# A gated Flamingo block on one core: the last two batch elements' ternary layers taken off GpSimd, their steps set apart, and reductions behind GpSimd pinned to their place

## The chip, the cores and the metric

The kernel runs on one core of a Trainium2 chip. A core has five engines that matter here: TensorE (PE; its weight loads, PEld, overlap its matmuls), VectorE (DVE), ScalarE (ACT), GpSimd (POOL) and SyncE (SP), which here only issues DMAs. Every engine works through its own queue in order; an instruction that waits for another engine holds up all that stands behind it on its own. The metric is the device time of one execution in microseconds (us); lower is better.

## The reference, cut to what matters

Four batch elements `x[b]` of 512 rows and 512 columns go through four layers, each added to the residual stream with a gate `tanh(g)`:

```python
x = x + tanh(g_xattn[0]) * wkv(layernorm(x), ctx)          # a scan over the rows
x = x + tanh(g_ffn[0])   * bitlinear_ffn(layernorm(x))     # 512 -> 2048 -> 512, 1-bit weights
x = x + tanh(g_xattn[1]) * attention(layernorm(x), ctx)    # 16 heads; int8-rounded projections
x = x + tanh(g_ffn[1])   * ternary(layernorm(x))           # RMS norm, int8 rounding, 512x512
```

The change is in the last two lines. The attention ends in a projection of its output, per row: the row's largest magnitude gives a scale, the row is rounded to integers, multiplied with the integer weights `wp`, rescaled and added to `x`. The ternary layer does nearly the same: normalise a row (`layernorm`, then RMS norm), multiply by `gamma`, take the largest magnitude, round to integers, multiply with ternary weights, rescale, add to `x`, write out.

## The kernel before, in words

**Tiles and lines of work.** One element `xb` is four tiles `t` of 128 rows x 512 columns. The work is written as Python generators ("lines"), each for one layer of one element, that yield after every small step. `run` (L1158) always advances the line whose next step has the smallest `place`; a line's `parts` say over which stretch of places its steps are spread. Places are counted in slots: `SLOTS = NT * NF + 1 = 17` slots to one element's feed-forward layer. So element b's attention runs beside element b+1's feed-forward layer, and the last element's attention (`alone`, b = 3) runs beside nothing but what is left of element 2: its `project_out` and its ternary layer. After the last attention unit only element 3's own end is left (`end`, L1045): `project_out` and `ternary` for tiles 0 and 1, and a step behind them for tiles 2 and 3.

**Who sets the order.** The matmuls and transposes of TensorE are chained to each other in the order of the steps (`in_turn`, `next_turn`, L153 to L165), so TensorE's order is the written one. On the other engines a scheduler in the build sets the order, by its own estimate of when operands are ready; `tc.keep_in_program_order(ins)` takes one instruction out of that freedom: it stays behind the instruction that was written just ahead of it on its engine. Before the change only some `bn_stats` have this (`pinned=True` in `layernorm`, L209).

**The attention** works in units of one head pair and half of the rows (`units`, L925; 16 units an element). Each unit has four score matmuls (`s_ps`), a row maximum on VectorE (`at_nm`, L938), an exponential on ScalarE (`at_P`, L940), sixteen transposes (`pt_ps`), copies of them out of PSUM on ScalarE (L960) or, for the last element, half of them on VectorE (L958), the product with the values (`o_ps`, one group of matmuls a unit) and a small collecting step (L998). `prepared` (L850) makes the rounded queries of a tile: normalise on GpSimd (`centred_aside`, L228), largest magnitude on VectorE (`absmax`, L231), round on ScalarE (`rounded`, L246), transpose on TensorE.

**`project_out`** (L1015), a tile: `absmax` of the output row block, scale, `rounded`; four transposes (`qr_ps`) and a copy; four matmuls (`p_ps`); then on VectorE `at_y` (L1031), and the addition to `xb` (L1032) on VectorE for the last element and on GpSimd for the others.

**`ternary`** (L1103), a tile, from statistics made by `layernorm(..., rms=True)`: for elements 0 to 2 the row is normalised on GpSimd (L228) and multiplied by `gamma` there (L1110); for element 3 on ScalarE (L224) and VectorE. Then on VectorE `absmax` (L231) and four small operations on one column (L1115 to L1118) that give the scale; `rounded` on ScalarE (L246); four transposes (`qr_ps`), a copy out (L253), four matmuls (`f_ps`), the addition to `xb` (L1128) and the DMA out. `layernorm` itself is per tile a `bn_stats` (L207) and a `bn_aggr` (L210), then for all of its tiles together two small operations for the variance (L213, L214), eleven of `rsqrt` (L182: a first guess by integer arithmetic and three Newton rounds of three operations each) and two that form scale and offset (L219, L220).

**Places.** Element b's attention ends at `end`; its `project_out` takes the six steps up to `end + 2.4` slots, and the ternary layer of elements 0 and 1 the seven steps from `end + 3` to `end + 8` slots, that of element 2 from `end + 4.5` to `end + 12` slots, with `aside=True` (each step late in its slot).

Of the kernel before, what the change touches and what calls it, by code (L numbers as in the profile page):

```python
# [10 lines left out]
F32 = mybir.dt.float32  # L11
# [10 lines left out]
P = 128  # L22
# [8 lines left out]
def kernel(  # L31
# [150 lines left out]
    def rsqrt(v, n):  # L182
# [13 lines left out]
            y = y2  # L196
        return y

    def layernorm(xb, rms=False, tiles=range(NT), pinned=False):

        n = len(tiles)
        mv = sm.tile([P, n, 2], F32, name="mv", tag="mv")
        for i, t in enumerate(tiles):
            s6 = sm.tile([P, 6], F32, name="s6", tag="s6")
            stats = nc.vector.bn_stats(s6, xb[:, t, :])  # L207
# [12 lines left out]
        nc.vector.scalar_tensor_tensor(r[:, 1, :], mv[:, :, 0], -1.0, y, ALU.mult, ALU.mult)  # L220
        return {t: (r[:, 0, i : i + 1], r[:, 1, i : i + 1]) for i, t in enumerate(tiles)}
# [5 lines left out]

        nc.gpsimd.tensor_scalar(dst, xb[:, t, :], r[t][0], r[t][1], ALU.mult, ALU.add)  # L228

    def absmax(dst, src):  # L230
        nc.vector.tensor_reduce(dst, src, AX.X, ALU.max, apply_absolute_value=True)  # L231

    def quantise(dst, src, rscale, lo, hi=127.0):

# [596 lines left out]
    def attention_layer(b, xb, pool, tiles=range(NT)):  # L831
# [18 lines left out]
        def prepared(t, r):  # L850
            xn = row("at_xn")
            centred_aside(xn, xb, r, t)
            s = sm.tile([P, 2], F32, name="at_s", tag="at_s")
            yield True
            absmax(s[:, 0:1], xn)
            int8_scale(s[:, 0:1], s[:, 1:2], s[:, 0:1])
            rounded(xn, s[:, 1:2])
            yield True
            transposed_rows(xqT[:, :, t * P : (t + 1) * P], xn)
            sp = bank("sx_ps")[:, 0:P]  # L860
            transpose(sp, s[:, 0:1].to_broadcast([P, P]), ident)
# [153 lines left out]
        def project_out(t):  # L1015
            s = sm.tile([P, 2], F32, name="at_s", tag="at_s")
            o = o_all[:, t, :]
            absmax(s[:, 0:1], o)
            int8_scale(s[:, 0:1], s[:, 1:2], s[:, 0:1])
            rounded(o, s[:, 1:2])  # L1020
            yield True
            oqT = pool.tile([P, NC, P], BF16, name="at_oqT", tag="at_oqT")
            transposed_rows(oqT, o)
            yield True
            pp = bank("p_ps")
            for c in range(NC):
                matmul(
                    pp, lhsT=oqT[:, c, :], rhs=wpT[:, c, :], start=(c == 0), stop=(c == NC - 1)
                )
            y = row("at_y")  # L1030
            nc.vector.scalar_tensor_tensor(y, pp, s[:, 0:1], swp_b, ALU.mult, ALU.mult)  # L1031
            (nc.vector if alone else nc.gpsimd).tensor_tensor(  # L1032
                xb[:, t, :], xb[:, t, :], y, ALU.add
            )
            yield True
# [9 lines left out]
        def end(ts):  # L1045

            yield from together([project_out(t) for t in ts])
            r = layernorm(xb, rms=True, tiles=ts)
            yield from together([ternary(b, xb, pool, t, r) for t in ts])


        ahead, behind_it = end((0, 1)), end((2, 3))
# [47 lines left out]
            yield from in_steps([project_out(t) for t in tiles], 1)  # L1100


    def ternary(b, xb, pool, t, r):  # L1103

        last = b == NB - 1
        if r is None:
            r = layernorm(xb, rms=True, tiles=[t])
        xn = pool.tile([P, D], F32, name="tf_xn", tag="at_row", bufs=ROWS)
        (centred if last else centred_aside)(xn, xb, r, t)
        (nc.vector if last else nc.gpsimd).tensor_tensor(xn, xn, gamma_b, ALU.mult)  # L1110
        s = sm.tile([P, 3], F32, name="tf_s", tag="tf_s")
        if not last:
# [15 lines left out]
        nc.vector.scalar_tensor_tensor(xt, fp, s[:, 2:3], xt, ALU.mult, ALU.add)  # L1128
# [238 lines left out]
```

## Time and profile before

| | |
|---|---|
| time, median of 3 runs | 1129.53 us (1128.88 to 1131.5) |
| the profiled execution: its own time | 1129.12 us |
| its span, first to last instruction | 1127.3 us |
| mean granted TensorE clock | 0.954 of full |
| busy, share of the span | PE 85%, DVE 78%, ACT 64%, POOL 27% |
| the last element's attention and the end | from about 955 us to the end |
| the end alone, after the last attention unit | from about 1089 us to the end |

The span is 1.82 us shorter than the execution's own time, and this execution is 0.41 us under the median. Busy shares are averages over stages with different limits; what one stage is worth has to be read in that stage. In the lines of the profile, `L171` is the transposing helper and `L168` the matmul helper, so those go by their tiles (`qr_ps`, `pt_ps`, `p_ps`, `f_ps`). Similarly L231 is `absmax` and L246 `rounded`, wherever they are called.

### The profile page before, as it was taken

The page shows a single profiled execution, that of the slowest core. Times are in us where ns is not written, and L with a number is a line of the kernel's source. Part 1 is how long each engine was busy: PE and PEld are TensorE (multiplying, and loading weights), DVE is VectorE, ACT ScalarE, POOL GpSimd, SP SyncE. Part 2 cuts the span into 40 slices and gives each one's busy share as a digit, 9 for nine tenths or more (in the row PEclk, how much of TensorE's full clock was granted, in tenths as well). Part 3 has the DMA queues.
Part 4 walks back from the last instruction along what each step waited for, and adds up shares of the span by engine and source line. Part 5 has one row for each costly group of instructions (what it writes and reads, how often), then busy time and mean ns, then how long its engine had stood idle before and what let it go on. Part 6 is the DMA issues. An engine that isn't in the chain of part 4 may idle for free.

```text
span 1127.3 us, 16575 instructions
## 1 busy us (share of the span) xinstructions
PE 962.9 (85%) x5548; PEld 678.1 (60%) x5548; DVE 877.7 (78%) x1885; ACT 721.4 (64%) x1482; POOL 308.8 (27%) x301
## 2 busy tenths in 40 slices
PE   3878898988878978899998797999999899888983
PEld 2344565555546656676776475777777677555651
DVE  5857547769877799998769899978689766688776
ACT  5677655453224677667767676777676677877763
POOL 3821004333104143531215536212122400112000
PEclk9888999998888999999999999999999999998996
DMA  8188854443434654645555554464674572333401
GB/s 279 38 291 302 295 193 150 177 177 149 149 120 151 225 189 155 217 159 175 191 187 182 164 182 169 152 208 150 218 214 146 187 233 60 113 104 104 130 2 38
DMA packets 85668, 189.58 MB, mean 168 GB/s; under 512 B 12240, under 2 KB 36816, under 8 KB 74576
## 3 DMA queue, kind: packets, MB, share of 16 engines
q1 hardware_dynamic: 85584, 188.53, 49.7%
q8 instruction: 44, 0.72, 0.3%
q14 instruction: 40, 0.33, 0.1%
HBM read 148.65 MB, written 39.85 MB: 167 GB/s over the span
## 4 chain that ended last, share of the span: by engine, by line
PE 43%; DVE 29%; ACT 13%; issue 5%; POOL 4%; DMA 4%; SPq 1%; ACTq 0%; POOLq 0%; DVEq 0%
PE ff_hp L168 13%; PE ff_acc L168 6%; PE pt_ps L171 5%; PE o_ps L168 4%; DVE at_nm L938 3%; PE v_ps L168 3%; DVE wk_q L631 3%; PE s_ps L168 3%; ACT at_P L940 3%; DVE qg_i L671 2%; PE tp_ps L171 2%; ACT at_PT L960 2%; PE qr_ps L171 2%; ACT wk_e L603 1%; DMA wn<-in_L_ffn_w_dram 1%
## 5 line engine op out<-in xcount | busy, mean ns | idle before, releaser
L168 PE MATMUL ff_hp<-wT,xp 128*128 128x512 f32 x1024 | 272.3, 410 | 3.1 <-ACT at_P L940 2.1
L168 PEld LDWEIGHTS ff_hp<-wT,xp 128*128 128x128 f32 x1024 | 195.4, 195 | 51.9 <-ACT at_P L940 4.4
L940 ACT ACTIVATE at_P<-s_ps,at_nm 128x512 f32<-128x512 f32 x256 | 174.8, 690 | 64.8 <-DVE at_nm L938 63.4
L938 DVE TENSOR_REDUCE at_nm<-s_ps 128x1 f32<-128x512 f32 x256 | 165.8, 677 | 27.1 <-PE s_ps L168 26.7
L676 POOL TENSOR_TENSOR ff_z<-qg_b,qg_s 128x512 f32<-128x512 bf16 x64 | 71.2, 1112 | 378.9 <-ACT qg_b L675 326.3
L171 PE MATMUL pt_ps<-ident,at_P 128*128 128x128 f32 x1024 | 142.0, 279 | 12.5 <-ACT at_os L980 5.1
L960 ACT COPY at_PT<-pt_ps 128x512 f32<-128x512 f32 x224 | 125.0, 596 | 39.1 <-PE pt_ps L171 38.4
L171 PEld LDWEIGHTS pt_ps<-ident,at_P 128*128 128x128 f32 x1024 | 113.9, 141 | 54.7 <-issue 13.9
L168 PE MATMUL ff_acc<-wT,hr 128*128 128x512 f32 x512 | 136.7, 408 | 6.3 <-DVE hr L688 3.3
L168 PE MATMUL s_ps<-at_kR,at_qR 128*128 128x512 f32 x256 | 97.2, 448 | 19.9 <-ACT at_P L940 12.7
L168 PEld LDWEIGHTS ff_acc<-wT,hr 128*128 128x128 f32 x512 | 92.4, 190 | 27.4 <-DVE hr L688 4.6
L736 ACT ACTIVATE ff_z<-ff_hp,coef 128x512 f32<-128x512 f32 x64 | 43.9, 686 | 68.7 <-PE ff_hp L168 65.6
L168 PE MATMUL o_ps<-at_PT,at_V 128*32 128x256 f32 x1024 | 72.6, 397 | 1.6 <-ACT at_PT L960 0.9
L675 ACT CAST qg_b<-qg_i 128x512 bf16<-128x512 int8 x80 | 49.4, 617 | 34.2 <-DVE qg_i L671 24.7
L741 DVE SCALAR_TENSOR_TENSOR ff_z<-ff_hp,coef,ff_z 128x512 f32<-128x512 f32 x64 | 47.6, 744 | 28.3 <-PE ff_hp L168 28.1
L168 PE MATMUL v_ps<-wkvT,cT 128*128 128x512 f32 x128 | 63.4, 643 | 5.0 <-DVE wT L318 1.8
L168 PEld LDWEIGHTS s_ps<-at_kR,at_qR 128*128 128x128 f32 x256 | 45.6, 194 | 35.9 <-ACT at_P L940 20.7
L168 PE MATMUL k_ps<-cT,wkvT 128*128 128x512 f32 x128 | 62.3, 637 | 3.1 <-ACT cT L455 1.4
L737 DVE SCALAR_TENSOR_TENSOR ff_z<-ff_z,ff_hp 128x512 f32<-128x512 f32 x64 | 43.5, 679 | 25.7 <-ACT ff_z L736 25.7
L687 ACT CAST hr<-tp_ps 128x512 fp32r<-128x512 f32 x64 | 37.6, 588 | 33.9 <-PE tp_ps L171 33.9
L631 DVE RECIPROCAL wk_q<-wk_q 128x256 f32<-128x256 f32 x32 | 54.3, 1718 | 1.4 <-POOL wk_p L619 1.4
L171 PE MATMUL tp_ps<-ident,ff_z 128*128 128x128 f32 x256 | 40.3, 281 | 14.9 <-ACT at_PT L960 5.8
(177 smaller groups left out, 1749.7 us busy)
## 6 DMA issues: line engine op xcount, KB each, us to landing
wT<-wD SPq DMA_DIRECT2D x72, 1024.0 KB, 5.3
wn<-in_L_ffn_w_dram SPq DMA_DIRECT2D x18, 1024.0 KB, 7.3
at_kR<-kD SPq DMA_DIRECT2D x128, 128.0 KB, 3.5
at_qR<-qD SPq DMA_DIRECT2D x256, 64.0 KB, 2.2
wD<-wT SPq DMA_DIRECT2D x12, 1024.0 KB, 4.5
kD<-k_half SPq DMA_DIRECT2D x16, 512.0 KB, 3.3
qD<-at_half SPq DMA_DIRECT2D x32, 256.0 KB, 2.1
cn<-in_ctx_dram SPq DMA_DIRECT2D x8, 512.0 KB, 5.9
```

The costliest lines, as they stand in the source:

```text
L168: return in_turn(nc.tensor.matmul(*args, **kwargs))
L171: return in_turn(nc.tensor.transpose(*args))
L631: nc.vector.reciprocal(half, half)
L675: nc.scalar.copy(qb, qi)
L676: nc.gpsimd.tensor_tensor(grouped(src), grouped(qb), s.unsqueeze(2).to_broadcast([P, NG, GS]), ALU.mult)
L687: nc.scalar.copy(part[:, 0, :], pt)
L736: nc.scalar.activation(z, hp, AF.Tanh, scale=coef[:, 0:1])
L737: nc.vector.scalar_tensor_tensor(z, z, 1.0, hp, ALU.add, ALU.mult)
L741: nc.vector.scalar_tensor_tensor(z, hp, coef[:, 1:2], z, ALU.mult, ALU.mult)
L938: nc.vector.tensor_reduce(nm, sp, AX.X, ALU.max, negate=True)
L940: nc.scalar.activation(lanes[k, i, t], sp, AF.Exp, bias=nm, accum_out=sums[k][:, t, i : i + 1],)
L960: made[k] = nc.scalar.copy(dst, blocks(pt))
```

## The change

1. **Element 2 and 3, the addition in `project_out`.** The addition to `xb` is on VectorE for both (it was on GpSimd for element 2), and `at_y` gets a buffer of another pool instead of one of the three row buffers that the attention uses.
2. **Element 2 and 3, statistics.** A new function `statistics` in place of `layernorm`: pinned `bn_stats`, the same `rsqrt`, but the mean and the scale are handed on apart. For element 3's tiles 2 and 3 the three Newton rounds are done on GpSimd, four operations each (`rsqrt_aside`).
3. **Element 2 and 3, the ternary layer.** One VectorE instruction, `(x - mean) * gamma`, takes the place of the normalising and the multiplication; it and the magnitude don't need the scale, which enters only the small column operations afterwards. Buffers come from pools that the feed-forward layer has left. The step that ended after the GpSimd work is gone.
4. **Element 2's places.** `project_out` is spread from `end - 0.15` to `end + 4.65` slots (to `end + 2.4` before), the ternary layer from `end + 4.85` to `end + 11.85` slots without `aside`; its statistics are a step of their own.
5. **Elements 0 and 1, and all of `prepared`.** `absmax` of what GpSimd has made, and the `bn_stats` of the ternary layer, are pinned to their place.

```diff
+    def rsqrt_aside(v, n):
+        half = sm.tile([P, n], I32, name="rs_half", tag="rs_half")
+        nc.vector.tensor_scalar(half, v.bitcast(I32), 1, None, ALU.logical_shift_right)
+        y = sm.tile([P, n], F32, name="rs_y", tag="rs_y")
+        nc.vector.tensor_scalar(y.bitcast(I32), half, -1.0, float(0x5F3759DF), ALU.mult, ALU.add)
+        for _ in range(3):
+            t = sm.tile([P, n], F32, name="rs_t", tag="rs_t")
+            nc.gpsimd.tensor_tensor(t, v, y, ALU.mult)
+            nc.gpsimd.tensor_tensor(t, t, y, ALU.mult)
+            nc.gpsimd.tensor_scalar(t, t, -0.5, 1.5, ALU.mult, ALU.add)
+            y2 = sm.tile([P, n], F32, name="rs_y", tag="rs_y")
+            nc.gpsimd.tensor_tensor(y2, y, t, ALU.mult)
+            y = y2
+        return y
...
-    def absmax(dst, src):
-        nc.vector.tensor_reduce(dst, src, AX.X, ALU.max, apply_absolute_value=True)
+    def absmax(dst, src, pinned=False):
+        ins = nc.vector.tensor_reduce(dst, src, AX.X, ALU.max, apply_absolute_value=True)
+        if pinned:
+            tc.keep_in_program_order(ins)
...
 # prepared
-            absmax(s[:, 0:1], xn)
+            absmax(s[:, 0:1], xn, pinned=True)
...
 # project_out
-            y = row("at_y")
+            if b > NB - 3:
+                y = wk.tile([P, D], F32, name="at_y", tag="wk_v")
+            else:
+                y = row("at_y")
             nc.vector.scalar_tensor_tensor(y, pp, s[:, 0:1], swp_b, ALU.mult, ALU.mult)
-            (nc.vector if alone else nc.gpsimd).tensor_tensor(
+            (nc.vector if b > NB - 3 else nc.gpsimd).tensor_tensor(
                 xb[:, t, :], xb[:, t, :], y, ALU.add
             )
...
 # end
-            r = layernorm(xb, rms=True, tiles=ts)
-            yield from together([ternary(b, xb, pool, t, r) for t in ts])
+            means, scale = statistics(b, xb, ts)
+            yield from together([ternary(b, xb, pool, t, means, scale) for t in ts])
...
+    def statistics(b, xb, tiles):
+        n = len(tiles)
+        mv = sm.tile([P, n, 2], F32, name="mv", tag="mv")
+        for i, t in enumerate(tiles):
+            s6 = sm.tile([P, 6], F32, name="s6", tag="s6")
+            tc.keep_in_program_order(nc.vector.bn_stats(s6, xb[:, t, :]))
+            nc.vector.bn_aggr(mv[:, i, :], s6)
+        v = sm.tile([P, n], F32, name="ln_v", tag="ln_v")
+        nc.vector.tensor_scalar(v, mv[:, :, 1], LN_EPS, RMS_EPS, ALU.add, ALU.mult)
+        nc.vector.tensor_tensor(v, v, mv[:, :, 1], ALU.add)
+        y = rsqrt_aside(v, n) if b == NB - 1 and tiles[0] else rsqrt(v, n)
+        m = sm.tile([P, n], F32, name="ln_m", tag="ln_m")
+        nc.vector.tensor_scalar(m, mv[:, :, 0], -1.0, None, ALU.mult)
+        at = {t: slice(i, i + 1) for i, t in enumerate(tiles)}
+        return {t: m[:, at[t]] for t in tiles}, {t: y[:, at[t]] for t in tiles}
...
 # ternary
-        last = b == NB - 1
-        xn = pool.tile([P, D], F32, name="tf_xn", tag="at_row", bufs=ROWS)
-        (centred if last else centred_aside)(xn, xb, r, t)
-        (nc.vector if last else nc.gpsimd).tensor_tensor(xn, xn, gamma_b, ALU.mult)
+        last = b > NB - 3
+        if last:
+            xn = ff.tile([P, D], F32, name="tf_xn", tag="ff_a", bufs=3)
+        else:
+            xn = pool.tile([P, D], F32, name="tf_xn", tag="at_row", bufs=ROWS)
...
+        if last:
+            nc.vector.scalar_tensor_tensor(xn, xb[:, t, :], r[t], gamma_b, ALU.add, ALU.mult)
+            absmax(s[:, 0:1], xn)
+            nc.vector.tensor_scalar(s[:, 0:1], s[:, 0:1], scale[t], 1e-5, ALU.mult, ALU.add)
+        else:
+            centred_aside(xn, xb, r, t)
+            nc.gpsimd.tensor_tensor(xn, xn, gamma_b, ALU.mult)
             yield True
-        absmax(s[:, 0:1], xn)
-        nc.vector.tensor_scalar(s[:, 0:1], s[:, 0:1], 1e-5, None, ALU.add)
+            absmax(s[:, 0:1], xn, pinned=True)
+            nc.vector.tensor_scalar(s[:, 0:1], s[:, 0:1], 1e-5, None, ALU.add)
         nc.vector.reciprocal(s[:, 1:2], s[:, 0:1])
-        nc.vector.tensor_scalar(s[:, 1:2], s[:, 1:2], 127.0, None, ALU.mult)
+        if last:
+            nc.vector.tensor_scalar(s[:, 1:2], s[:, 1:2], scale[t], 127.0, ALU.mult, ALU.mult)
+        else:
+            nc.vector.tensor_scalar(s[:, 1:2], s[:, 1:2], 127.0, None, ALU.mult)
...
-        xT = pool.tile([P, NC, P], BF16, name="tf_xT", tag="at_oqT")
+        if last:
+            xT = ring.tile([P, NC, P], BF16, name="tf_xT", tag="w")
+        else:
+            xT = pool.tile([P, NC, P], BF16, name="tf_xT", tag="at_oqT")
...
 # ternary_layer
-        r = layernorm(xb, rms=True)
-        yield from in_steps([ternary(b, xb, pool, t, r) for t in range(NT)], 1)
+        if b == NB - 2:
+            r, scale = statistics(b, xb, range(NT))
+            yield
+        else:
+            r, scale = layernorm(xb, rms=True, pinned=True), None
+        yield from in_steps([ternary(b, xb, pool, t, r, scale) for t in range(NT)], 1)
...
 # the places of the lines
-            (end, end + 2.4 / SLOTS, 6),
+            (end, end + 2.4 / SLOTS, 6)
+            if b != NB - 2
+            else (end - 0.15 / SLOTS, end + 4.65 / SLOTS, 6),
...
-                (end + (3 if b < NB - 2 else 4.5) / SLOTS, end + (8 if b < NB - 2 else 12) / SLOTS, 7),
-                aside=True,
+                (end + 3 / SLOTS, end + 8 / SLOTS, 7)
+                if b < NB - 2
+                else (end + 4.85 / SLOTS, end + 11.85 / SLOTS, 7),
+                aside=b < NB - 2,
```

Counted over the built programs, VectorE has 4 instructions fewer (1887 to 1883), ScalarE 4 fewer, GpSimd as many as before (12 of 128x512 go, 12 of 128x2 come), and TensorE and SP as many. TensorE's written order differs only in the stretch of element 2's `project_out`.

More of the change, by code (lines that the diff above doesn't have):

```diff
@@ L197, in rsqrt @@
         return y
+    def rsqrt_aside(v, n):
+        half = sm.tile([P, n], I32, name="rs_half", tag="rs_half")
+        nc.vector.tensor_scalar(half, v.bitcast(I32), 1, None, ALU.logical_shift_right)
+        y = sm.tile([P, n], F32, name="rs_y", tag="rs_y")
+        nc.vector.tensor_scalar(
+            y.bitcast(I32), half, -1.0, float(0x5F3759DF), ALU.mult, ALU.add
+        )
+        for _ in range(3):
[7 more added lines that the diff above has]
+        return y
     def layernorm(xb, rms=False, tiles=range(NT), pinned=False):
@@ L1100, in attention_layer @@
             yield from in_steps([project_out(t) for t in tiles], 1)
-    def ternary(b, xb, pool, t, r):
-        last = b == NB - 1
-        if r is None:
-            r = layernorm(xb, rms=True, tiles=[t])
-        xn = pool.tile([P, D], F32, name="tf_xn", tag="at_row", bufs=ROWS)
-        (centred if last else centred_aside)(xn, xb, r, t)
-        (nc.vector if last else nc.gpsimd).tensor_tensor(xn, xn, gamma_b, ALU.mult)
-        s = sm.tile([P, 3], F32, name="tf_s", tag="tf_s")
-        if not last:
+    def statistics(b, xb, tiles):
[13 more added lines that the diff above has]
+        return {t: m[:, at[t]] for t in tiles}, {t: y[:, at[t]] for t in tiles}
@@ new lines, in ternary @@
+    def ternary(b, xb, pool, t, r, scale=None):
+        last = b > NB - 3
[3 more added lines that the diff above has]
+            xn = pool.tile([P, D], F32, name="tf_xn", tag="at_row", bufs=ROWS)
+        s = sm.tile([P, 3], F32, name="tf_s", tag="tf_s")
+        if last:
+            nc.vector.scalar_tensor_tensor(
+                xn, xb[:, t, :], r[t], gamma_b, ALU.add, ALU.mult
+            )
+            absmax(s[:, 0:1], xn)
[3 more added lines that the diff above has]
+            nc.gpsimd.tensor_tensor(xn, xn, gamma_b, ALU.mult)
@@ L1113, in ternary @@
             yield True
-        absmax(s[:, 0:1], xn)
-        nc.vector.tensor_scalar(s[:, 0:1], s[:, 0:1], 1e-5, None, ALU.add)
+            absmax(s[:, 0:1], xn, pinned=True)
+            nc.vector.tensor_scalar(s[:, 0:1], s[:, 0:1], 1e-5, None, ALU.add)
         nc.vector.reciprocal(s[:, 1:2], s[:, 0:1])
-        nc.vector.tensor_scalar(s[:, 1:2], s[:, 1:2], 127.0, None, ALU.mult)
+        if last:
+            nc.vector.tensor_scalar(
+                s[:, 1:2], s[:, 1:2], scale[t], 127.0, ALU.mult, ALU.mult
+            )
+        else:
+            nc.vector.tensor_scalar(s[:, 1:2], s[:, 1:2], 127.0, None, ALU.mult)
```

## The prediction

> **What bounds the kernel now.** I read the waits first, because the change takes GpSimd out of the way of VectorE. Columns: waiting engine and line, whom it waited for, us in total, times, longest.
>
> ```profile
> DVE tf_s L231 <- POOL tf_xn L1110: 6.0, 6, 2.3
> DVE at_s L231 <- POOL at_xn L228: 4.4, 4, 1.7
> DVE s L207 <- POOL xb L1032: 3.2, 4, 1.4
> PE qr_ps L171 <- ACT tf_xn L246: 17.6, 4, 8.0
> PE qr_ps L171 <- ACT at_o L246: 7.6, 3, 3.4
> ```
>
> VectorE stands at a magnitude or a statistic until GpSimd has made the row; TensorE stands at the transposes of a row until it is rounded (14.0 of the 17.6 lie in the end, 3.6 in element 2). The waits are worth what stands behind them, so next the stages: windows cut at the starts of `o_ps`, one attention unit each. Columns: window, us, then busy us (and instructions) of PE, PEld, DVE, ACT, POOL, then granted clock, DMA share, GB/s.
>
> ```profile
> 982.03:998.01 15.98, 12.20 (x70) 7.57 (x69) 11.91 (x26) 12.97 (x31) 1.26 (x1) 0.83 0.52 162
> ...
> 1021.34:1026.66 5.32, 4.76 (x42) 3.19 (x41) 4.64 (x19) 4.21 (x13) 0.00 (x0) 1.00 0.72 209
> 1026.66:1036.64 9.98, 6.31 (x45) 4.20 (x45) 7.55 (x29) 6.05 (x16) 6.62 (x7) 0.84 0.36 104
> 1036.64:1044.41 7.77, 7.45 (x49) 4.99 (x49) 5.39 (x14) 5.86 (x15) 1.45 (x2) 0.77 0.00 0
> 1044.41:1050.60 6.19, 6.11 (x49) 4.03 (x48) 4.89 (x10) 5.43 (x14) 0.00 (x0) 1.00 0.28 87
> ```
>
> A plain unit takes 5.32 us; one that carries a tile of the ternary layer 6.19. Element 2's `project_out` (first row) and the start of its ternary layer (third and fourth) are far over that, at a lower clock. The timeline says why (start, us, engine, line, operation; in brackets the idle time before and its releaser):
>
> ```profile
> 883.75 0.69 DVE L231 TENSOR_REDUCE tf_s<-tf_xn 128x1 f32<-128x512 f32 x1 [2.26 <-POOL tf_xn L1110]
> ...
> 1034.51 0.69 DVE L231 TENSOR_REDUCE tf_s<-tf_xn 128x1 f32<-128x512 f32 x1 [0.72 <-POOL tf_xn L1110]
> 1034.74 1.12 PE L171 MATMUL qr_ps<-ident,tf_xn 128*128 128x128 f32 x4 [3.59 <-ACT tf_xn L246]
> ```
>
> Last the end, in the chain of waits (start, us, what):
>
> ```profile
> 1102.19 0.82 ACT tf_xn L224
> ...
> 1108.03 0.82 ACT tf_xn L246
> ...
> 1113.72 0.82 ACT tf_xn L224
> ...
> 1117.59 0.82 ACT tf_xn L246
> ...
> 1123.20 0.75 DVE xb L1128
> ```
>
> From the first `at_y` (1095.05) to 1113.7 the chain is VectorE nearly throughout, step after step: statistics and Newton rounds of tiles 0, 1, their rows, then the same for tiles 2, 3.
>
> **Prices.** On VectorE a 128x512 operation occupies 0.60 us (L207 at 1097.10, L1032 at 1097.70), 0.66 from PSUM, and its dependent starts 0.76 after it; a column operation occupies 0.07, its dependent starts 0.20 later (1099.36, 1099.56). A rounding is 0.82, four cold transposes 1.1, the copy 0.7, four cold `f_ps` matmuls 1.4, the last addition 0.75.
>
> **The end.** In the built order VectorE now runs, from 1095.05: four `at_y` (2.64), and fourteen 128x512 operations (8.4): four additions, four `bn_stats`, three rows, three magnitudes. In between stand about 23 column operations, mostly free to follow at once: 2.3. So the guess for tiles 2, 3 is there at 1095.05 + 13.35 = 1108.4. The roundings of tiles 0, 1 start about 1109.0 and 1109.7, 2.4 and 1.7 us later than before; that costs nothing as long as their TensorE work (done about 1114.5) is ahead of tile 3's. Then twelve dependent GpSimd steps, while VectorE stands at the first column operation that needs their scale; queued behind it are the whole of tile 3's row and magnitude, so the wait is on the path. The trace has no GpSimd arithmetic of two columns. Nearest rows: its 128x1 memset, 0.10, plus 0.08 between dependent GpSimd operations (884.95 for 0.78, next at 885.81): 0.18 a step. From above: 1.27 and 0.77 for 128x512, with the 0.08 1.35 and 0.85: nine and three of them, 14.7 in all. I take 0.25, near the memset because the size is near: 3.0 us, so 1111.45. Behind it: column operations 0.55, row 0.75, magnitude 0.7, column operations 0.55 (2.55), rounding 0.82, transposes 1.1, copy 0.7, `f_ps` 1.4, addition 0.75, handoffs 0.1: 7.4. The last addition ends at 1118.85, not 1123.95: **-5.1**. The bounds: 0.18 gives -5.9, 14.7 gives +6.6; the turning point is 0.67 a step.
>
> The rule that speaks against this step is in the Trainium skill, GPSIMD Engine Reference, section 3.1: elementwise work belongs on VectorE, since a GpSimd instruction passes two software dispatch hops. From its 4497 ns for 2048 elements at 2.5 to 2.6 cycles of 1.2 GHz I estimate 0.06 to 0.23 us of fixed cost; by that the twelve steps would take about 0.7 to 2.8 us, and no row here shows it. The page also names contention with VectorE for SBUF; here VectorE stands still meanwhile.
>
> **Element 2, project_out.** GpSimd loses four additions (1.28 each), VectorE gains them: 4 x 0.60 = 2.4. It loses the four `bn_stats` here (2.7), which move to the ternary layer's first step. So VectorE's load is about even, and the 2.9 us in which TensorE waited for a rounded `at_o` inside 982 to 998, and the 1.8 in which VectorE waited for GpSimd's addition, are spread away. The 2.6 us wait for `at_qR`'s DMA at 979 stays. TensorE in a plain unit: 4.76; transposes add 0.45, `p_ps` 1.0, `q_ps` 0.95. The six units from 982.03 to 1026.66 took 44.6. In the new order they carry: transposes, `q_ps` and one more score pair (9.8; before, that far took 9.3); two tiles' transposes and products (7.8); one (6.3); `p_ps` and `q_ps` (6.7); nothing (5.35, twice): 41.3, **-3.3**. Bounds: 0 if VectorE fills the units (it is busy 5.26 of 5.35 in 1015.99 to 1021.34), -8 if all over the plain sum goes.
>
> **Element 2, ternary layer.** GpSimd loses 4 x 0.774 and 4 x 1.287. VectorE gains four rows, 2.5, and the four `bn_stats`. Six units from 1021.34 to 1062.88 took 41.5. After: the statistics lengthen one unit to 6.5; the next, with a row and a magnitude, 6.1; then the built order has three rows, two magnitudes and about eleven column operations ahead of a row maximum, 4.5 us during which the exponentials and TensorE run dry: 8.5; then 6.5, 6.3, 5.9: 39.8, **-1.7**, bounds +3 (that block as long as today's 9.98 and 7.77 stay, statistics on top) and -4. The new row from two SBUF tiles has no row of its own; its neighbours are 0.69 (L1110) and 0.75 (L1128).
>
> **Elements 0 and 1.** From 880 to 906 VectorE waits 5.1 us for GpSimd's rows, and TensorE 3.6 behind it (3.2 at one place). Pinned, these magnitudes come after their unit's own work. The first tile's stands about 1.3 us of VectorE work behind the scale, while GpSimd needs 0.77 + 1.29: a new wait of 0.8, queued behind it a row maximum. 3.6 less 0.8, less something for later roundings: **-2.0**, bounds -3.6 and +2. At element 0's layer (655 to 700) VectorE is busy 44.5 of 45 and waits for no GpSimd row, so there only the new 0.8 counts; in `prepared` three waits of 0.9 go. Together **0**, bounds -3 and +3.
>
> Sum: -5.1 - 3.3 - 1.7 - 2.0 = -12.1; 1129.1 - 12.1 = 1117.0 for an execution like the profiled one, and 0.4 more for the median: **1117.4**. Its own range, with the middle values of the bounds, is 1111 to 1122.
>
> **Rivals.**
> *VectorE is the bound of the last attention* (20%): it gains 4.9 us of 128x512 work there, the units are 90% and more VectorE, and what GpSimd's waits give, the work takes back. Then the end alone counts: 1124.4. For it: 5.37 of 5.63 in 1005.00 to 1010.63. Against it: 4.7 to 4.9 of about 6 in the units from 1044 on.
> *Pinned magnitudes make TensorE wait for roundings* (13%), the case on the other side. A magnitude that stands at its place comes later, its rounding too, and TensorE's order is fixed. `project_out`'s magnitudes are late already, and there TensorE waits 7.6 us for 16 tiles, 0.48 a tile; for `prepared` only 3.4, for elements 0 and 1's ternary rows nothing. 24 tiles are newly pinned. From 0.5 us a tile it eats the whole 12.1; at 0.7 it costs 16.8: 1134.1. Against it: those rows have a unit or more of lead.
> *GpSimd's small steps cost like large ones* (7%): +6.6 in place of -5.1: 1129.1, no change. Against it: the 0.10 memset.
> *More than the sum* (10%): with the waits gone the clock stays at 1.00 from 980 to 1050 and the 11 us that TensorE idles or runs slow there go as well: about 1110.
>
> Clock: the rows above show 0.84 and 0.77 after a wait of 3.6 us. The Trainium skill, TensorE: Matmul & The Clock Gate, Part 1, puts the limit at an idle window of about 3.4 us; if waits stay under it, 1.3 us of the 7.77 unit's matmuls would go in any case, which is inside the sum above.
>
> **Numbers.** The forecast 50%: 1117.4. A measurement of this kernel can tell 0.2%, 2.3 us, from no change. Faster: the forecast, the first and the last rival, less a little that ends near zero: 0.77. Same: the third and that little: 0.09. Slower: 0.14. From 1109 to 1130 only most of the second rival and half of the last are left out.
>
> **What would show it.** After: no VectorE wait for `tf_xn` or `xb` by GpSimd past 950 us; units from 982 to 1063 of 8.5 at most but the first; GpSimd steps of 0.2 to 0.3 in the end, about 24 us from the first `at_y` to the last addition (28.9 before). Wrong if `qr_ps` waits for `tf_xn` or `at_xn` grow before 950, if units with rows stay at 8 to 10 us, or if GpSimd's steps are over 0.67.

## The result, and the profile after

The change makes the kernel slower: 1150.9 us, median of 5 runs (1146.66 to 1153.12), against 1129.65 us (1128.88 to 1132.19) for the kernel before beside it. The ratio is 1.0168, with a 95% interval of 1.0138 to 1.0199; the forecast was 1117.4, and its range ended at 1130. The profiled execution, the slowest of the five, has a span of 1151.3 us (1127.3 before) and a mean granted clock of 0.938 (0.954).

In the changed kernel's lines, `absmax` is L250 (L231 before), `rounded` L267 (L246), the normalising on GpSimd L246 (L228). First the waits, the answer to the five lines that the prediction began with (waiting engine and line, whom it waited for, us in total, times, longest):

```profile
DVE tf_s L250 <- POOL tf_xn L1162: 4.5, 3, 2.2
DVE at_s L250 <- POOL at_xn L246: 0.9, 1, 0.9
PE qr_ps L171 <- ACT tf_xn L267: 25.0, 5, 11.0
PE qr_ps L171 <- ACT at_xn L267: 7.9, 3, 4.2
PE qr_ps L171 <- ACT at_o L267: 4.7, 2, 3.4
```

The change does what it says: VectorE's waits for GpSimd's rows fall from 13.6 us to 5.4 (2.6 come new, for the Newton rounds in the end). But TensorE's waits for a rounded row grow from 28.6 (17.6, 7.6 and the 3.4 of `at_xn`) to 37.6. These totals can't say where the 24 us of span went, because a wait early in TensorE's order delays everything behind it.

So I matched the TensorE instructions of the two traces, which are the same ones in nearly the same order, and took for each how much later it starts than in the trace of before. That difference rises in steps. Table 1 gives the steps by stage (us, worked out from the starts in the traces; the columns are stages in the time of before). The lower rows are the experiments that follow. Where exactly a stage is cut moves a step by up to 0.9 us.

| kernel | 340 to 385: element 0's queries | 660 to 710: element 0's ternary layer | 860 to 900: element 1's ternary layer | 977 to the end: elements 2 and 3 |
|---|---|---|---|---|
| after | +6.2 | +12.3 | +3.2 | -2.9 |
| e2: before with the pins | +5.8 | +11.8 | +3.1 | -1.5 |
| e11: before, the four pins on element 0's queries alone | +5.7 | +2.9 | +1.3 | -2.2 |
| e3: after, queries free | -0.2 | +10.1 | +4.8 | -2.4 |
| e4: after, layers free | +6.5 | 0.0 | -0.2 | -4.6 |
| e5: after, statistics free | +6.3 | +1.7 | +2.6 | -2.4 |
| e6: after, magnitudes free | +6.1 | +7.9 | +0.5 | -2.6 |
| e1: after, no pins | +1.3 | +1.3 | +1.3 | -4.6 |

How far these numbers can be trusted shows in stages where a kernel's instructions are unchanged. In the eight kernels with nothing pinned at the ternary layers (e1, e4, and e7 to e12 below) the two middle columns come out between 0 and +3.0, and between -0.2 and +1.4. The first 130 us, where all orders are the same, come out between -0.4 and +3.8, and the last column with the code of before in it (e2, e11) at -1.5 and -2.2. So steps up to 3 us are the spread of executions; 5.7 and 12 are not. Of the -2.9 of after in the last column, all but about 1 lies within what unchanged code shows there.

**Element 0's queries.** Before, the first two magnitudes of the queries ran at 347.33, as soon as GpSimd had made the rows (start, us, engine, line, operation; in brackets the idle time before, and its releaser):

```profile
347.33 1.27 DVE L231 TENSOR_REDUCE at_s<-at_xn 128x1 f32<-128x512 f32 x2
...
350.92 1.12 PE L171 MATMUL qr_ps<-ident,at_xn 128*128 128x128 f32 x4 [2.16 <-ACT at_xn L246]
```

The timeline of after:

```profile
348.30 1.53 POOL L246 TENSOR_SCALAR at_xn<-xb,ln_r 128x512 f32<-128x512 f32 x2 [3.02 <-DVE ln_v L234]
...
349.80 2.51 POOL L885 TENSOR_TENSOR xb<-xb,bp_b 128x512 f32<-128x512 f32 x2
349.81 1.29 DVE L187 TENSOR_SCALAR rs_y<-rs_half 128x2 int32<-128x2 int32 x1
351.13 1.19 DVE L192 SCALAR_TENSOR_TENSOR rs_t<-rs_y,ln_v 128x2 f32<-128x2 f32 x1
...
353.93 0.17 DVE L237 COPY ln_r<-rs_y 128x2 f32<-128x2 f32 x1
...
354.68 0.68 DVE L250 TENSOR_REDUCE at_s<-at_xn 128x1 f32<-128x512 f32 x1
...
356.69 1.12 PE L171 MATMUL qr_ps<-ident,at_xn 128*128 128x128 f32 x4 [4.20 <-ACT at_xn L267]
...
378.24 0.65 PE L171 MATMUL qr_ps<-ident,at_xn 128*128 128x128 f32 x4 [2.48 <-ACT at_xn L267]
```

The first two rows are ready by 349.83. The magnitude stands until 354.68, because the instructions written ahead of it are the first guess and the three Newton rounds of the *next* two tiles, which end at 354. Two of these take 1.29 and 1.19 us in place of 0.16, each while a GpSimd addition on 128x512 runs beside it; that is 2.2 of the 4.85 us. TensorE, with its fixed order, waits 4.20 us, 2.16 before, and at 378.24 it waits 2.48 more, for the fourth tile's rounding; it has no such wait there before. These two waits give 4.5 of the step of 6.2.

**Element 0's ternary layer.** Here the pinned `bn_stats` put the Newton rounds late, from 675 to 688 us (657 to 663 before; after is already some 12 us behind when the layer begins), and there GpSimd works on element 2's scan. Timeline of after:

```profile
680.90 2.06 POOL L648 TENSOR_TENSOR wk_e<-wk_e,wk_v 128x512 f32<-128x512 f32 x1
681.82 1.15 DVE L195 SCALAR_TENSOR_TENSOR rs_y<-rs_t,rs_y 128x4 f32<-128x4 f32 x1
...
682.92 1.78 POOL L653 TENSOR_TENSOR wk_e<-wk_e,wk_p 128x512 f32<-128x512 f32 x1
683.50 1.22 DVE L192 SCALAR_TENSOR_TENSOR rs_t<-rs_y,ln_v 128x4 f32<-128x4 f32 x1
...
685.38 1.12 PE L171 MATMUL pt_ps<-ident,at_P 128*128 128x128 f32 x4 [3.73 <-DVE hr L709]
...
699.51 2.51 POOL L1162 TENSOR_TENSOR tf_xn<-tf_xn,gamma_b 128x512 f32<-128x512 f32 x2
...
718.79 0.67 DVE L250 TENSOR_REDUCE tf_s<-tf_xn 128x1 f32<-128x512 f32 x1
...
722.41 1.11 PE L171 MATMUL qr_ps<-ident,tf_xn 128*128 128x128 f32 x4 [6.16 <-ACT tf_xn L267]
```

An operation on four columns, 0.15 elsewhere, takes 1.15 and 1.22, and each ends within 0.02 us of the GpSimd operation beside it (682.97 and 682.96; 684.72 and 684.70). Behind them in VectorE's queue stands `hr` (L709), and TensorE waits 3.73 for it. Later the magnitude of the third tile, whose row was ready at 702.02, stands at its place until 718.79, and TensorE waits 6.16 for its rounding. Before, the magnitudes of the third and fourth tile ran together, 3.4 us after the third row:

```profile
687.10 1.24 DVE L231 TENSOR_REDUCE tf_s<-tf_xn 128x1 f32<-128x512 f32 x2
```

A third wait of TensorE, 3.47 us at 705.33, ends with VectorE's `xb` (L665). How much of the 12.3 lies in these waits, and how much in the lower clock behind them (see the end of the account of the prediction), I did not separate.

**Element 1's ternary layer** shows the same in small: the third tile's row is ready at 911.62, its magnitude runs at 917.71, and the transposes wait 3.56. The step of 3.2 is at the edge of the spread.

```profile
909.06 2.56 POOL L1162 TENSOR_TENSOR tf_xn<-tf_xn,gamma_b 128x512 f32<-128x512 f32 x2
...
917.71 0.68 DVE L250 TENSOR_REDUCE tf_s<-tf_xn 128x1 f32<-128x512 f32 x1
...
921.28 0.66 PE L171 MATMUL qr_ps<-ident,tf_xn 128*128 128x128 f32 x4 [3.56 <-ACT tf_xn L267]
```

**Element 2.** Windows cut at the starts of `o_ps`, as in the prediction (window, us, busy us of PE, PEld, DVE, ACT, POOL, then clock, DMA share, GB/s). These are the first unit of `project_out`, the unit with the statistics, the unit with the first rows, and the one behind it:

```profile
1009.12:1019.63 10.51, 8.34 (x54) 5.33 (x53) 8.23 (x14) 8.74 (x23) 0.00 (x0) 0.87 0.50 160
...
1045.86:1052.12 6.26, 5.23 (x42) 3.25 (x41) 6.26 (x19) 4.39 (x12) 0.00 (x0) 1.00 0.76 205
1052.12:1062.82 10.70, 6.15 (x46) 4.44 (x45) 10.63 (x41) 6.86 (x16) 0.00 (x0) 0.85 0.30 79
1062.82:1070.13 7.31, 7.31 (x49) 5.05 (x48) 5.81 (x16) 6.12 (x14) 0.00 (x0) 0.75 0.04 9
```

The first came down from 15.98 to 10.51. The unit with the first rows is as long as before (9.98, now 10.70), with VectorE busy 10.63 of it; TensorE stands 3.82 in it, at a transpose.

**The end**, in the chain of waits (start, us, what):

```profile
1134.86 0.21 POOL rs_t L209
...
1137.68 0.19 POOL rs_t L211
...
1139.60 0.67 ACT tf_xT L274
1140.32 3.60 PE f_ps L168 x8
1143.92 0.87 PE qr_ps L171 x4
...
1147.49 0.75 DVE xb L1186
```

The twelve GpSimd steps take 0.20 each with 0.28 from one to the next, 3.3 us in all. The chain then does not go on through tile 3's row, magnitude and rounding, but over the copies of tiles 0 and 1 (`tf_xT`) and their products. From the first `at_y` (1121.06) to the start of the last addition it is 26.43, against 28.16 before. The forecast's 23.8 counts to the end of that addition, 0.75 later: 27.18 by the same count, against 28.91 before.

### The profile page after: what moved, and what is told of

Its sections match the earlier page's. It is cut to its first block, busy times and chain, and to the rows that moved or that the text cites. A ratio compares the mean times of both kernels' runs of the same rounds, so it can differ in the third digit from the quotient of the medians.

```text
span 1151.3 us, 16567 instructions
## 1 busy us (share of the span) xinstructions
PE 975.3 (85%) x5548; PEld 686.4 (60%) x5548; DVE 886.2 (77%) x1881; ACT 721.0 (63%) x1478; POOL 299.5 (26%) x301
## 4 chain that ended last, share of the span: by engine, by line
PE 48%; DVE 25%; ACT 13%; issue 5%; DMA 4%; POOL 3%; SPq 1%; POOLq 0%; ACTq 0%; DVEq 0%
PE ff_hp L168 14%; PE ff_acc L168 7%; PE pt_ps L171 6%; PE o_ps L168 4%; PE s_ps L168 4%; PE v_ps L168 3%; ACT at_P L961 3%; DVE wk_q L652 3%; DVE at_nm L959 2%; DMA wn<-in_L_ffn_w_dram 2%; PE tp_ps L171 2%; PE qr_ps L171 2%; DVE qg_i L692 2%; ACT at_PT L981 1%; ACT wk_e L624 1%
## 5 line engine op out<-in xcount | busy, mean ns | idle before, releaser
L168 PEld LDWEIGHTS ff_hp<-wT,xp 128*128 128x128 f32 x1024 | 198.0, 197 | 52.7 <-ACT at_P L961 4.5
L959 DVE TENSOR_REDUCE at_nm<-s_ps 128x1 f32<-128x512 f32 x256 | 166.6, 678 | 40.2 <-PE s_ps L168 39.8
L171 PE MATMUL pt_ps<-ident,at_P 128*128 128x128 f32 x1024 | 144.7, 281 | 18.0 <-ACT at_os L1001 4.9
L168 PE MATMUL ff_acc<-wT,hr 128*128 128x512 f32 x512 | 140.8, 417 | 6.3 <-DVE hr L709 3.3
L168 PE MATMUL s_ps<-at_kR,at_qR 128*128 128x512 f32 x256 | 99.7, 457 | 19.7 <-ACT at_P L961 14.4
L168 PEld LDWEIGHTS ff_acc<-wT,hr 128*128 128x128 f32 x512 | 95.4, 196 | 28.2 <-DVE hr L709 4.6
L168 PE MATMUL v_ps<-wkvT,cT 128*128 128x512 f32 x128 | 65.9, 664 | 4.8 <-DVE wT L339 1.8
L961 ACT ACTIVATION_READ_ACCUMULATOR at_P<-s_ps,at_nm 128x1 f32 x256 | 51.9, 203 | 0.0
```

The costliest lines, as they stand in the source:

```text
L168: return in_turn(nc.tensor.matmul(*args, **kwargs))
L171: return in_turn(nc.tensor.transpose(*args))
L959: nc.vector.tensor_reduce(nm, sp, AX.X, ALU.max, negate=True)
L961: nc.scalar.activation(lanes[k, i, t], sp, AF.Exp, bias=nm, accum_out=sums[k][:, t, i : i + 1],)
```

## The experiments

In these runs the kernel before took 1125.8 to 1139.0 us, with medians of 1131 to 1133, so times are read by their ratio to the kernel before that ran beside them.

### Which part costs it: e1 to e4

**e1**, no pins:

```diff
-            absmax(s[:, 0:1], xn, pinned=True)          # prepared; ternary of elements 0, 1
+            absmax(s[:, 0:1], xn)
-            r, scale = layernorm(xb, rms=True, pinned=True), None
+            r, scale = layernorm(xb, rms=True), None
```

> Part 5 of the change undone (no reduction of elements 0 and 1 or of the rounded queries is pinned); parts 1 to 4 stay. Theory A, the pins cost it: matched instruction by instruction on TensorE, the changed kernel is 26.9 us behind at the start of the last attention and 24.0 behind at its end, so parts 1 to 4 give 2.9 back: about 1126.7. Rival B, the edits of elements 2 and 3 cost it (their rows on VectorE, their buffers taken from other pools): still 1145 or more. Rival C, my forecast of the end and of element 2 was right and hidden: 1119.

Measured: 1130.42 us, ratio 0.9986 (0.9964 to 1.0008). B and C fall, A holds.

**e2**, the kernel before with the pins alone (`pinned=True` in `prepared`, and `pinned=b < NB - 2` in the ternary layer's `layernorm` and `absmax`):

> The kernel before with part 5 alone: the sixteen magnitudes of the rounded queries, and the statistics and magnitudes of the ternary layers of elements 0 and 1, pinned; elements 2 and 3 as before. Theory A: 1129.6 + 26.9 less about 3 that the profiled run lost in its first 130 us, where nothing is pinned: 1151 to 1156. Rival B: 1135 at most.

Measured: 1150.96 us, ratio 1.0188 (1.0145 to 1.0231). That is the lower edge of A's range: the pins alone make the whole loss.

**e3**, the changed kernel, queries free:

```diff
-            absmax(s[:, 0:1], xn, pinned=True)          # prepared
+            absmax(s[:, 0:1], xn)
```

> The changed kernel with the magnitudes of the rounded queries not pinned; the pins of the ternary layers of elements 0 and 1 stay. Theory A, the two kinds add: the steps of 6.0 us (at 346 to 379 us of before, element 0's queries) and 2.8 us (437 to 512, element 1's) go: 1150.9 - 8.8 = 1142. Rival D, the large step at 666 to 707 us belongs to element 2's queries, which lie there too: 1130. Rival E, the kinds cover for one another: 1148 or more.

Measured: 1143.44 us, ratio 1.014 (1.0094 to 1.0186). The step at 340 to 385 is gone (-0.2), those of the layers stay. D falls by the time; the interval alone would still admit E, but E has no place for a step that is gone.

**e4**, the changed kernel, `layernorm` and `absmax` of the ternary layers of elements 0 and 1 free:

> The changed kernel with the statistics and magnitudes of the ternary layers of elements 0 and 1 not pinned; those of the rounded queries stay. Theory A: the steps of 12.7 us (666 to 707 us of before) and 3.4 us (870 to 895) go: 1150.9 - 16.1 = 1135. Rival D, the step at 666 to 707 belongs to element 2's queries: 1147. Rival E: 1148 or more.

Measured: 1138.07 us, ratio 1.0036 (1.0003 to 1.0068), nearer to A than to any rival; the steps at 660 and 860 us are gone (0.0 and -0.2), the one at 340 stays (+6.5). The two kinds add.

### Statistics or magnitudes: e5, e6

**e5** takes `pinned=True` from the `layernorm` of the ternary layers alone, **e6** from their `absmax` alone.

> The changed kernel with the statistics of the ternary layers of elements 0 and 1 not pinned; their magnitudes, and those of the rounded queries, stay pinned. In the changed kernel's trace the first row of element 0's layer is normalised at 688.5 us, 12.4 us later than before once the 12.3 us by which the kernel is behind there are taken off. Theory A1, the pinned statistics put their whole chain late: the two steps at elements 0 and 1 (11.5 and 3.2 us) go: 1150.9 - 14.7 = 1136. Theory A2, the pinned magnitudes do it: 1149 or more. Both share it: 1143.

> The mirror of the run above: the magnitudes of the ternary layers of elements 0 and 1 not pinned, their statistics pinned, and the rounded queries' magnitudes too. Theory A1: 1149 or more. Theory A2: 1136. Both share it: 1143.

Measured: e5 1140.55 us, ratio 1.0074 (1.0048 to 1.0101); e6 1146.34 us, 1.0119 (1.0087 to 1.0151). By the medians both share it, but not in the same places. At element 0's layer the pinned statistics alone make 7.9 us, the pinned magnitudes alone 1.7, which lies within the spread, both together 12.3; at element 1's layer it is 0.5 and 2.6. So the share of the statistics at element 0's layer is shown; that of the magnitudes shows only on top of it (4.4 us), and the intervals of e5 and e4, and of e6 and after, overlap a little. TensorE's waits in the stretch of element 0's layer, first of e5, then of e6:

```profile
PE qr_ps L171 <- ACT tf_xn L267: 4.7, 1, 4.7
```

```profile
PE pt_ps L171 <- DVE hr L709: 3.7, 1, 3.7
PE pt_ps L171 <- DVE xb L665: 3.5, 1, 3.5
```

With the magnitudes pinned TensorE waits for one late rounding. With the statistics pinned it waits for VectorE's other work behind the Newton rounds. Of the latter, I did not separate how much is lateness and how much the long operations beside GpSimd.

### One pin alone: e11

**e11**: the kernel before (there `rounded` is now L248), with `absmax(s[:, 0:1], xn, pinned=b == 0)` in `prepared`.

> The kernel before with one pin alone: the four magnitudes of element 0's rounded queries. Theory: these stood behind the statistics and the Newton rounds of the next two tiles, and TensorE's transposes behind them; the step of 5.3 to 6.5 us between 340 and 385 us is there, the pins on the other elements' queries cost nothing (the step of 2.8 at 437 to 512 was no part of it): 6 over the kernel before. Rival, the pins on elements 1 to 3 carry a share: 3 or less.

Measured: 1139.91 us, ratio 1.0057 (1.0035 to 1.0079): 4 to 9 us over the kernel before, by the interval. The step of 5.7 is there, and its line of the timeline is like that of after:

```profile
355.22 1.11 PE L171 MATMUL qr_ps<-ident,at_xn 128*128 128x128 f32 x4 [3.97 <-ACT at_xn L248]
```

So four magnitudes carry what the pinned queries cost; the twelve of the other elements show no step beyond the spread.

### The end: e7, e8, e9

**e7** is e1 with the Newton rounds on VectorE:

```diff
-        y = rsqrt_aside(v, n) if b == NB - 1 and tiles[0] else rsqrt(v, n)
+        y = rsqrt(v, n)
```

> The first experiment's kernel (no pins of part 5) with the Newton rounds of the last two tiles on VectorE, nine operations in place of twelve on GpSimd. In the first experiment's trace the twelve took from 1112.38 to 1115.67, 3.3 us, and VectorE stood still for 2.6 of them. My forecast's theory, moving them aside costs nothing that VectorE would not wait for anyway: the end alone (37.07 us from the start of the last o_ps) within 0.5 of that. Rival, the aside steps are the chain: nine at 0.20 are 1.8 us, so the end is 1.5 shorter, 35.6; and if ScalarE's order turns round with it (copies of tiles 0 and 1 ahead of tile 2's rounding), up to 3.4 shorter, 33.7.

**e8** is e1 with GpSimd's Newton rounds, and a step and a pin on ScalarE (`rounded` hands its instruction to `tc.keep_in_program_order`):

```diff
+        behind = b == NB - 1 and t > 1
+        if behind:
+            yield True
-        rounded(xn, s[:, 1:2])
+        rounded(xn, s[:, 1:2], pinned=behind)
```

> The first experiment's kernel with one step between: ScalarE's two copies of tiles 0 and 1 come ahead of the rounding of tile 2, three instructions of ScalarE in another order and nothing else. In the first experiment's trace the copies are ready at 1114.9 and start at 1117.12, behind a rounding that waits for GpSimd's scale. Theory: the f_ps of tiles 0 and 1 start 2.1 us sooner, and the end becomes 35.1 (37.07 before). Rival, the chain runs through tile 3's rounding (1118.53) in any case: within 0.4 of 37.07.

Measured: e7 1127.08 us, ratio 0.9957 (0.9931 to 0.9982); e8 1127.76 us, 0.9969 (0.9947 to 0.9992). Counted from the last `o_ps` the ends are 34.55 and 35.74, but of these the part ahead of the first `at_y`, the same instructions in both, takes 6.5 and 7.6. From the first `at_y` on, the end repeats to 0.04 us over the six kernels that share its order, so Table 2 counts from there, to the start of each (us):

| | roundings, tiles 0, 1 | copies, tiles 0, 1 | roundings, tiles 2, 3 | first `f_ps` | last addition |
|---|---|---|---|---|---|
| before | 11.53, 12.98 | 13.70, 15.06 | 22.54, 23.26 | 14.76 | 28.16 |
| after | 14.37, 15.09 | 18.54, 19.11 | 17.82, 19.96 | 19.26 | 26.43 |
| e8 | 14.36, 15.08 | 16.38, 17.23 | 17.82, 19.94 | 17.12 | 24.04 |
| e7 | 14.40, 15.12 | 16.42, 17.71 | 17.00, 19.06 | 17.16 | 23.92 |

In after, ScalarE takes tile 2's rounding ahead of the two copies, stands 1.93 us for the scale that GpSimd makes, and the copies stand behind it: they start at 18.54, where in e8 they start at 16.38. Against e1, which ends at 26.44, e8 differs in the order of these three instructions and nothing else, so they are worth 2.4 us. Timelines, first of after, then of e8:

```profile
1138.88 0.81 ACT L267 ACTIVATE tf_xn<-tf_xn,magic,tf_s 128x512 f32<-128x512 f32 x1 [1.93 <-DVE tf_s L1168]
...
1139.60 1.24 ACT L274 ACTIVATE tf_xT<-qr_ps,magic 128x512 bf16<-128x512 f32 x2
```

```profile
1114.76 0.69 ACT L276 ACTIVATE tf_xT<-qr_ps,magic 128x512 bf16<-128x512 f32 x1 [0.50 <-PE qr_ps L171]
...
1116.20 0.81 ACT L267 ACTIVATE tf_xn<-tf_xn,magic,tf_s 128x512 f32<-128x512 f32 x1
```

And the place of the Newton rounds hardly matters once the copies come first: on VectorE tile 2's rounding is 0.82 sooner, the last addition 0.12. In e7 the order of ScalarE turned round by itself with the edit, as the rival there said it might, and that is most of its gain.

**e9**: the kernel before with element 3's edit alone, Newton rounds on VectorE.

> The kernel before with element 3's edit alone (statistics apart, one VectorE row, scale in the column operations), its Newton rounds on VectorE; element 2 and all places as before, nothing pinned. Theory: the end is its own, 34.55 us from the last o_ps as in the run with Newton on VectorE (38.80 before): 4.2 less than the kernel before, 1127 against 1131 on this chip. Rival, the end's gain needs element 2's edit too (VectorE free of it when the end begins): 37 or more. What lies between this run and the run with Newton on VectorE is element 2's edit.

Measured: 1129.04 us, ratio 0.9972 (0.9952 to 0.9992); last addition 23.54 after the first `at_y`. The end's gain of 4.6 is its own. Element 2's edit makes no difference between e7 and e9 that their intervals could tell.

### Element 2's ternary layer: e10, e12

**e10** is e7 with element 2's roundings one step later:

```diff
+        if b == NB - 2:
+            yield True
         rounded(xn, s[:, 1:2])
...
-                else (end + 4.85 / SLOTS, end + 11.85 / SLOTS, 7),
+                else (end + 4.85 / SLOTS, end + 12.85 / SLOTS, 8),
```

> The run with Newton on VectorE (no pins), and element 2's roundings and transposes one step (one slot) later, eight steps in place of seven. There the unit with the first rows takes 10.0 us, TensorE standing 3.8 at a transpose. Theory F, the transposes' written place is too early: the unit falls to 6.3, and the whole is 3.7 shorter than that run. Theory G, VectorE is the bound there (busy 9.93 of 10.00; 27.7 of 30.1 over four units): at most 2.4 goes, and the units are full of VectorE wherever the transposes stand.

**e12** is e7 with element 2's ternary layer (`layernorm`, rows and `gamma` on GpSimd) as before (`aside=True` too), at the new places.

> The run with Newton on VectorE (no pins), with element 2's ternary layer as before (rows and gamma on GpSimd) at its new places; project_out's addition stays on VectorE at its new places. Theory G, VectorE is the bound of that layer: the unit of the statistics and the 10.0 unit lose the rows (4 x 0.6 on VectorE), GpSimd's 2.1 us a row comes back as a wait: the six units from 1024.9 to 1066.9 of the first experiment (42.0) stay within 1. Theory F: GpSimd's wait is longer and comes on top: 44 or more. My forecast's theory (rows on VectorE save 1.7): 43.7.

Measured: e10 1125.0 us, ratio 0.9934 (0.991 to 0.9957); e12 1131.49 us, 0.9999 (0.9972 to 1.0025). The statistics' unit and the two behind it in e10, then the unit of the first rows in e7 and in e12:

```profile
1029.70:1035.96 6.26, 5.22 (x42) 3.25 (x41) 6.26 (x19) 4.39 (x12) 0.00 (x0) 1.00 0.73 204
1035.96:1041.90 5.94, 4.97 (x42) 3.47 (x41) 5.94 (x21) 4.49 (x13) 0.00 (x0) 1.00 0.21 62
1041.90:1048.84 6.94, 5.00 (x46) 3.60 (x45) 6.94 (x22) 5.76 (x16) 0.00 (x0) 1.00 0.37 107
```

```profile
1029.56:1039.65 10.09, 5.54 (x46) 3.88 (x45) 10.02 (x40) 6.78 (x16) 0.00 (x0) 0.97 0.34 86
```

```profile
1030.16:1045.04 14.88, 6.17 (x46) 4.22 (x45) 9.23 (x35) 7.10 (x17) 6.60 (x7) 0.73 0.25 69
```

The unit falls from 10.09 to 5.94, and the seven units from the statistics on, up to the same `o_ps`, take 43.5 in e10 and 47.3 in e7 (47.4 before): 3.8 less, theory F's 3.7 and more than theory G's 2.4. The times alone can't decide between the two: by the ratios e10 is 0.23%, some 2.6 us, under e7, and their intervals overlap. The transposes stood in TensorE's order a unit ahead of what VectorE could make. What G said of the rest holds too: in the three units of e10 VectorE is busy all of the time, so it is now the likely bound. In e12 the rows on GpSimd make the unit 14.88, with a wait of 8.71 at the transposes; the six units take 45.9 against 42.0, as theory F had it, so at these places element 2's edit of its ternary layer (row, statistics and the place of each step in its slot together) is worth 3.9.

e10 has the lowest ratio of all: 0.66% under the kernel before (0.43% to 0.90%), which the changed kernel exceeds by 1.68%.

## Why the prediction was wrong, point by point

**The step that failed is the one on elements 0 and 1**, priced at -2.0 and 0 with upper bounds of +2 and +3 us. It measured +3 and +18 (6 at element 0's queries, 12 at its ternary layer); the pins alone cost 21 us (16 to 26) by e2. The other three steps failed too, by less: without the pins (e1) they gave 1.6 us together (from 4.1 gained to 0.9 lost) in place of 10.1. Three things went wrong in the step on elements 0 and 1. I priced a pinned magnitude by its new wait for GpSimd (0.8 us). What it costs is everything written ahead of it: three Newton rounds for the next two tiles at the queries' first magnitude, and up to 17 us of other work for the third tile of element 0's layer. I did not price the pinned `bn_stats` at all, though the diff names them, and they make the larger part at element 0's layer (e6). And I took "VectorE is busy 44.5 of 45 there" as a reason why a pin could gain nothing, and did not ask what it could cost: a full engine has little room to make up for work that comes late. That last is an argument; no run tests it, and at element 0's queries VectorE was busy for only 24.9 of 32.6 us (346 to 379 of before). At element 1's layer the wait that the step was to remove did shrink, from 3.6 us to 1.6 (TensorE behind the copies `at_PT`), and a new one of 3.56 came in its place.

**The second rival had the mechanism**: pinned magnitudes come later, their roundings too, and TensorE's order is fixed. I priced it as an even 0.7 us a tile (1134.1). The runs show it uneven: 1.4 a tile at element 0's queries, nothing that shows at the other twelve query tiles, and about 1.9 a tile for the eight rows of the ternary layers, the statistics included. What I held against it, "those rows have a unit or more of lead", is false for element 0's queries, where TensorE waited 2.16 even before. Two of the prediction's own signs of being wrong came true: `qr_ps` waits for `at_xn` grew from 3.4 to 7.9 us, and the unit with the first rows stayed above 10.

**The end**: forecast 23.8 from the first `at_y` to the end of the last addition, measured 27.18; a gain of 5.1 was forecast and 1.7 came. The terms were near: scale chain ready for GpSimd at 13.35, measured 13.80; twelve steps 3.0, measured 3.3; tile 3's rounding at 18.95, measured 19.96. What failed is the sentence that the later roundings of tiles 0 and 1 cost nothing "as long as their TensorE work (done about 1114.5) is ahead of tile 3's". It was done 22.9 after the first `at_y`, not 19.5, since I took VectorE's order from the built program and did not look at ScalarE's. With that order turned (e8) the end measures 24.79 by the same count.

The Trainium skill, GPSIMD Engine Reference, section 3.1, was weighed there. The row that was lacking is now in the trace: 0.20 busy and 0.28 from step to step, a little over the 0.7 to 2.8 us that I estimated from the page for the twelve. Its advice costs nothing to follow here: e7 and e8 are 0.12 apart.

**Element 2's `project_out`**: forecast 44.6 to 41.3, measured 43.0 (42.7 in e1). The units went the way that the sum said (10.5, 7.6, 6.7, 6.1, 5.9 for 9.8, 7.8, 6.3, 6.7, 5.35), but with unchanged code these six take 44.2 in e2 and 42.8 in e9, so little of it can be called a gain. I also counted the unit from 1021 to 1027 twice: at 5.35 here, and at 6.5 with the statistics in the next sum.

**Element 2's ternary layer**: forecast 39.8, measured 42.4 (41.5 before). The unit with the first rows and the next one were put at 14.6 together; they take 18.0. I saw that VectorE would be full and still let TensorE's transposes go at their place. The first rival, VectorE as the bound, looks nearer here (10.63 of 10.70), but e10 shows that the transposes' place carried 3.8 us of it.

**The clock**: the waits of 3.73, 3.47 and 6.16 at element 0's layer were followed by stretches at 0.50; that of 3.56 at element 1's layer by 1.00. Windows of after behind the last of these and the first two (the clock stands behind POOL's column):

```profile
921.30:927.00 5.70, 5.70 (x43) 4.01 (x44) 2.63 (x4) 3.92 (x9) 2.07 (x2) 1.00 0.42 112
...
685.40:689.00 3.60, 2.30 (x9) 1.90 (x10) 3.60 (x8) 2.12 (x6) 3.41 (x4) 0.50 0.29 92
...
705.30:709.00 3.70, 3.67 (x11) 3.09 (x12) 2.72 (x16) 3.44 (x7) 0.34 (x1) 0.50 0.02 4
```

So among waits of about 3.5 us the length alone doesn't decide it. That agrees with the Trainium skill, TensorE: Matmul & The Clock Gate, Part 1, which calls the window of about 3.4 us free-running, so that it matters where in it a wait falls. But the length that the prediction took from there as a limit was none: in before, a wait of 2.52 us at 699.43, with one of 1.29 just ahead of it, was followed by a clock of 0.59 over the next 3.6 us.

## What to carry to other kernels

An instruction that is pinned behind what was written ahead of it inherits all of that work's delay, so price a pin by reading what stands ahead of it on its engine, and by who waits behind it in an order that is fixed. When one engine's work is made faster or moved, read the new order of every engine on the chain: here 2.4 us hung on three instructions of ScalarE, which the edit never named. And when rows come later than their transposes, moving the transposes one step (3.8 us here) can be worth as much as taking their making to another engine (3.9).

## What the runs showed of the hardware

VectorE operations on a few columns were held for as long as a GpSimd operation on 128x512 ran beside them: 1.15, 1.22 and 0.82 us in place of 0.15 at element 0's layer, 1.29 and 1.19 at its queries, each ending within 0.02 us of a GpSimd operation's end. GpSimd's own operations took 1.78 and 2.06 there instead of 1.27. The Trainium skill, SBUF — State Buffer, section "Who interferes with whom", states it as an exclusive lock between VectorE instructions with two SBUF inputs and GpSimd instructions that read SBUF, held for the whole instruction; four of the five held operations have two such inputs, so there the traces agree. The fifth, the `tensor_scalar` of 1.29 us at 349.81, has one input, which the rule on two inputs doesn't cover; why it was held stays open. A chain of small steps is cheap in a stretch where GpSimd rests (0.20 a step), and dear beside its work.

GpSimd arithmetic on 128x2 takes 0.20 us, with 0.28 from one dependent step to the next.
